# The end of a one-core attention and recurrence kernel: a chain in written order, earlier banks, ten warm-up steps

## The chip, the cores and the metric

The kernel runs on one core of a Trainium2 chip. The metric is device time in microseconds (us), the median of several runs. The engines are TensorE (PE in the profile; PEld is its weight load), VectorE (DVE), ScalarE (ACT), GpSimd (POOL) and SyncE (SP, which here only issues transfers). Each works through a queue of its own in order, and they wait for each other by semaphores. Matrix products write to PSUM[...].

## The reference

The input x has shape (4, 128, 64, 64) in float32: four batches of 128 channels and 4096 positions. Two layers are computed.

```
x = x + conv_attn(group_norm(x))          # q, k of width 64; softmax attention over 4096 positions, gated
t = tokens of x                           # (4, 4096, 128)
t = t + attn(layer_norm(t))               # q = x W, scores q q^T, softmax, weighted sum
t = t + ffn(layer_norm(t))
    # ffn: Wx = t W^T, normalised over all 4*4096 rows (batch norm),
    #      y_i = sigmoid(Wx_i + V y_{i-1}), y_{-1} = 0, over the 4096 positions in order
```

Everything is float32. The last part is a recurrence over 4096 steps for four sequences. V is orthogonal.

## The kernel before

The function `fast` does the work; a function `general` follows it, which computes everything again in a plainer way and is entered only if a test on the device fails.

The four batches run one after the other. For each batch, `layer0` computes the first attention (scores L238, exponentials L240, weighted sums L476), and `layer1` the second. In `layer1` the queries equal the keys, so the score matrix is symmetric: only blocks on and under the diagonal are computed (L795, exponentials L801), weighted directly (L672), and used a second time in transposed form, after DVE's block transposes (L642), a transfer and `reversed_products` (L685). Each of the eight blocks of 512 positions is finished by three pieces of work: `tokens` (four transposes on PE, L727; the row sums and their reciprocal, L730 to L732; products with it, L734; a layer norm, L299 to L303, whose inverse square root is taken on POOL, L145 and L146), `turn` (four transposes of the normalised rows, L747, copied by ACT, L748, and the block's result sent to HBM, L275 and L279) and `inputs` (the product with the feed-forward weight, L756; its statistics, L757; and a copy to `wxs`, L760). These pieces lie in the queue `pending`, and one is taken after each pair of score products. Block 0 of the last batch is the very last to be finished: nothing but its own chain is left then.

The order of instructions on an engine is chosen by a scheduler from priorities, except where the code asks for written order: the start of the kernel (inside `written`), and single instructions.

Then comes the recurrence. It isn't run over 4096 steps in a row: each sequence is cut into G = 128 pieces of L = 32 steps, all pieces of all four batches go forward together, and each piece begins W = 12 steps early from a zero state; since the sigmoid and V contract, the state has converged when the piece proper begins. So there are 12 + 32 = 44 steps. A step handles two halves (two batches of 128 pieces, 256 columns each): DVE preloads a PSUM bank with the scaled input (`preload`, L949, two steps ahead, three banks for each half), PE adds the product with V and the state before (L962), and ACT takes the sigmoid with the bias (L966). [...]every bank is first written by one product of PE (L926, the six marking products)[...]. Step 0 has no product: ACT takes the sigmoid of `wxs` times gain plus bias (L959). `gain` and `bias` come from the statistics of all blocks (L930 to L935). From step W + 3 on, DVE also adds the states to `t2s` (L976), one addition of 512 elements per partition for a batch and four steps; `t2s` is loaded from HBM by four transfers (L915), and when a batch is complete it is sent to the output (L981). At the end the state of each piece is compared with the state that the piece before it ended with (`gap`), and the row sums of both attentions with two bounds (`ok`, L905 to L907); if one test fails, `general` runs.

The PSUM pools of `fast` are `ps_s` (two buffers of two banks, scores), `ps_o` (three banks) and `ps_m` (one bank). The recurrence's own pool of six banks, `ps_r`, opens after these have been closed.

At the start, four warm-up products (L857, identity times the first columns of x) run while x is loaded and its statistics are taken; one more stands after the group mean (L346) and two after the group variance (L356). The first normalisation is L362, the first product of the projections L369.

Of the kernel before, what the change touches and what calls it, by code (L numbers as in the profile page):

```python
# [23 lines left out]
NT = N // P  # L24
# [8 lines left out]
PAIRS = NT // 2  # L33
LAG = 2
SHIFT = 48.0
L, W = 32, 12
G = N // L
GB = QB // L

# [133 lines left out]
def fast(  # L173
# [10 lines left out]
    bias = keep.tile([P, 1], F32, name="bias")  # L184
    first_y = keep.tile([P, 1], F32, name="first_y")

    with ExitStack() as st:
        big = st.enter_context(tc.tile_pool(name="big", bufs=1))
        ep = st.enter_context(tc.tile_pool(name="ep", bufs=4))
        accp = st.enter_context(tc.tile_pool(name="accp", bufs=1))  # L190
        work = st.enter_context(tc.tile_pool(name="work", bufs=1))
        stat = st.enter_context(tc.tile_pool(name="stat", bufs=4))
        ps_s = st.enter_context(tc.tile_pool(name="ps_s", bufs=2, space=PSUM))
        ps_o = st.enter_context(tc.tile_pool(name="ps_o", bufs=3, space=PSUM))
        ps_m = st.enter_context(tc.tile_pool(name="ps_m", bufs=1, space=PSUM))

# [96 lines left out]
        def layernorm(src, dst):  # L293

            mv = stat.tile([P, NQ, 2], F32, tag="mv", name="mv")
            rstd = stat.tile([P, NQ], F32, tag="rstd", name="rstd")
            for j in range(NQ):
                s6 = stat.tile([P, 6], F32, tag="s6", name="s6")
                nc.vector.bn_stats(s6, src[j])  # L299
                nc.vector.bn_aggr(mv[:, j, :], s6)  # L300
            inv_sqrt(rstd, mv[:, :, 1], EPS_LN)
            for j in range(NQ):
                nc.vector.tensor_scalar(  # L303
                    dst[j], src[j], mv[:, j, 0:1], rstd[:, j : j + 1],
                    ALU.subtract, ALU.mult,
                )
# [244 lines left out]
        def layer1(b, h, qt):  # L551
# [151 lines left out]
            def finish(n):  # L703
                cs = bass.ts(n, QB)
                rinv = stat.tile([P, NQ], F32, tag="rinv", name="rinv")
                t = work.tile([P, 4, NQ, 32], F32, tag="t", name="t1", bufs=2)
                if b == B - 1 and n == 0:

                    one, two = (ep.tile([P, 2, QB], F32, tag="e", name="last") for _ in range(2))
                    h2, t1 = (one[:, r, :].rearrange("q (j c) -> q j c", j=NQ) for r in range(2))  # L710
                    th = two[:, 0, :]

                    def bank():
                        return ps_s.tile([P, 2, QB], F32, tag="s", name="ml")[:, 0, :]
                else:
                    h2 = work.tile([P, NQ, C], F32, tag="h2", name="h2")
                    th = work.tile([P, QB], F32, tag="th", name="th")
                    t1 = work.tile([P, NQ, C], F32, tag="og", name="t1b")

                    def bank():  # L720
                        return ps_m.tile([P, QB], F32, tag="m", name="m1")
                nc.sync.dma_start(t, t_d[b, n])

                def tokens():
                    m = bank().rearrange("q (j c) -> q j c", j=NQ)
                    for j in range(NQ):
                        nc.tensor.transpose(m[:, j, :], oacc[:, n, bass.ts(j, P)], ident)  # L727
                    at = (B + b) * NT + n * NQ
                    den = den_all[:, at : at + NQ]
                    nc.vector.tensor_reduce(den, m, AX.X, ALU.add)  # L730
                    nc.vector.tensor_scalar(den, den, 1.0 / C, None, ALU.mult)
                    nc.vector.reciprocal(rinv, den)  # L732
                    for j in range(NQ):
                        nc.vector.scalar_tensor_tensor(  # L734
                            t1[:, j, :].rearrange("q (p i) -> q p i", p=4),
                            m[:, j, :].rearrange("q (p i) -> q p i", p=4), rinv[:, j : j + 1],
                            t[:, :, j, :], ALU.mult, ALU.add,
                        )
                    layernorm(quarters(t1), quarters(h2))

                def result():
                    turn_out(t1.rearrange("q j (p i) -> q j p i", p=4), t2_d[b, :, cs])

                def turn():
                    m = bank()
                    for j in range(NQ):
                        nc.tensor.transpose(m[:, bass.ts(j, P)], h2[:, j, :], ident)  # L747
                    nc.scalar.copy(  # L748
                        th.rearrange("c (p j k) -> c j p k", j=NQ, p=4),
                        m.rearrange("c (j p k) -> c j p k", j=NQ, p=4),  # L750
                    )
                    result()

                def inputs():
                    m = bank()
                    nc.tensor.matmul(m, lhsT=wt["f"], rhs=th, start=True, stop=True)  # L756
                    nc.vector.bn_stats(bn_st[:, b * NB + n, :], m)  # L757
                    m = m.rearrange("p (g i s) -> p i g s", i=L // 2, s=2)
                    if b == B - 1:
                        nc.vector.tensor_copy(wxs[:, :, b, bass.ts(n, GB), :], m)  # L760
                    else:
                        wx = work.tile([P, L // 2, GB, 2], F32, tag="wx", name="wx")
                        nc.vector.tensor_copy(wx, m)
                        nc.sync.dma_start(wxs_d[b, :, :, bass.ts(n, GB), :], wx)

                if b == B - 1 and n == 0:
                    pending.appendleft(tokens)
                    pending.extend([turn, inputs])
                elif b == B - 1 and n < 4:
                    pending.extend([tokens, turn, inputs])  # L770
                else:
                    pending.extend([tokens, nothing, nothing, nothing, turn, inputs])
# [66 lines left out]
                unsent.popleft()()  # L839
            while fifo:  # L840
                direct()
            pending.extend([reversed_products] * len(turned))

        def own_bank(_):
            return ps_m.tile([P, 512], F32, tag="m", name="mp")
# [8 lines left out]
        def warm(cols):  # L854

            m = ps_o.tile([P, QB], F32, tag="o", name="warm")
            nc.tensor.matmul(  # L857
                m[:, :cols], lhsT=ident, rhs=parts0[0][:, :cols], start=True, stop=True
            )

        for _ in range(4):
            warm(QB)
        for work_ in norm[:-2]:
            work_()
# [34 lines left out]
                ahead.popleft()()  # L899
        flush()  # L900


        tc.keep_in_program_order(nc.scalar.activation(first_y, shift, AF.Sigmoid))
        ok = big.tile([P, 2, 2 * B * NT], F32, tag="oacc", name="ok")
        nc.vector.tensor_scalar(ok[:, 0, :], den_all, DEN_LO, None, ALU.is_ge)  # L905
        nc.vector.tensor_scalar(ok[:, 1, :], den_all, DEN_HI, None, ALU.is_le)
        nc.vector.tensor_reduce(par_ok[:, 1:2], ok.rearrange("p a b -> p (a b)"), AX.X, ALU.min)  # L907


    with ExitStack() as st:  # L910
        scan = st.enter_context(tc.tile_pool(name="scan", bufs=1))
        ps_r = st.enter_context(tc.tile_pool(name="ps_r", bufs=1, space=PSUM))
        t2 = scan.tile([P, B, N], F32, name="t2s")
        for b in range(B):
            nc.sync.dma_start(t2[:, b, :], t2_d[b])  # L915
        y = scan.tile([P, L // 2, B, G, 2], F32, name="y")
        state = scan.tile([P, B, G + 1], F32, name="state")
        nc.gpsimd.memset(state[:, :, 0:1], 0.0)

        HB = B // 2
        banks = [[ps_r.tile([P, 512], F32, tag=f"r{s}{i}", name="ps_r") for i in range(3)] for s in range(2)]
        for s in range(2):
            for i in range(3):
                nc.tensor.matmul(  # L926
                    banks[s][i][:, : HB * G], lhsT=ident, rhs=wxs[:, 0, :HB, :, 0],
                    start=True, stop=True, skip_group_check=True,
                )
# [13 lines left out]
        def at(tile_, i, bs):  # L943
            return tile_[:, i // 2, bs, :, i % 2]
# [7 lines left out]
        preload(1)  # L952
        preload(2)
        for k, i in enumerate(steps):
            for s, bs in enumerate(halves):

                dst = state[:, bs, 1:] if k == W - 1 else at(y, i, bs)
                if k == 0:
                    nc.scalar.activation(dst, at(wxs, i, bs), AF.Sigmoid, bias=bias, scale=gain)  # L959
                    continue  # L960
                before = state[:, bs, :G] if k == W else at(y, i - 1, bs)
                nc.tensor.matmul(  # L962
# [7 lines left out]
            if k >= W:  # L970
                todo.extend((i - 3, b) for b in range(B) if i % 4 == 3)
                for j in range(len(todo) if i == L - 1 else min(1, len(todo))):
# [419 lines left out]
```

## Time and profile before

| | before |
|---|---|
| median of 3 runs | 3025.35 us (3024.1 to 3025.53) |
| profiled execution, its own time | 3023.71 us |
| its span, first to last instruction | 3021.6 us |
| PE busy | 2963.2 us, 98% of the span |
| DVE busy | 1718.1 us, 57% |
| ACT busy | 1017.0 us, 34% |
| POOL busy | 217.5 us, 7% |
| mean granted TensorE clock | 0.992 |

The profile is of one execution, so its durations belong to 3023.71 us and not to the median. In the chain of waits a line gives a start, a duration and what the end of the kernel hung on at that moment: engine, tile and line; "issue" is time in which an engine waited for nothing that the profile shows. A line of the timeline gives start, duration, engine, line, operation, output and inputs, their shapes, how many instructions were merged, and in brackets how long the engine had been idle and what released it. A line of the view by windows gives a stretch, its length, the busy time and the number of instructions of PE, PEld, DVE, ACT and POOL, then the granted clock (1.00 is full), the share of the DMA engines and GB/s. A busy PE is not PE at its peak, and a few matmul records may be missing. The ends of matmuls are modelled.

### The profile page before, as it was taken

The numbers are of one execution on the slowest core, as the hardware profiler recorded it, in microseconds if no ns is written. First come the engines' busy times: TensorE is split into PE (matmuls) and PEld (weight loads), VectorE is DVE, ScalarE is ACT, GpSimd is POOL, SyncE is SP. The second block draws the span as 40 slices with busy tenths as digits, with TensorE's granted clock in tenths as the row PEclk, the third lists the DMA queues.
The fourth block names the chain that finished last, engine by engine and source line by source line (L and its number), as shares of the span: only waits on it lengthen the run. The fifth ranks groups of instructions, "written<-read, shape, count | busy, mean of one in ns | idle before, by whom it ended". The sixth has DMA issues, their size and how long they took to land.

```text
span 3021.6 us, 32547 instructions
## 1 busy us (share of the span) xinstructions
PE 2963.2 (98%) x10768; PEld 1381.4 (46%) x10768; DVE 1718.1 (57%) x3210; ACT 1017.0 (34%) x1127; POOL 217.5 (7%) x215
## 2 busy tenths in 40 slices
PE   9999999999999999999999999999999999999985
PEld 4444444444444444444444444444444444444442
DVE  6666654544666664544466666454456666244446
ACT  3444422222344432232244443222234444222224
POOL 0011100000011100000011101000001101000000
PEclk9999999999999999999999999999999999999998
DMA  1111144334112124444311114443411113444433
GB/s 42 41 55 56 46 135 105 97 98 110 28 56 57 50 90 107 106 99 106 72 46 56 51 44 130 104 103 95 106 42 56 50 42 111 129 109 107 103 124 150
DMA packets 265425, 250.62 MB, mean 83 GB/s; under 512 B 96160, under 2 KB 180640, under 8 KB 264224
## 3 DMA queue, kind: packets, MB, share of 16 engines
q1 hardware_dynamic: 239328, 216.95, 26.6%
q10 hardware_dynamic: 25920, 31.49, 4.1%
q8 instruction: 89, 1.46, 0.2%
q14 instruction: 88, 0.72, 0.1%
HBM read 65.80 MB, written 56.62 MB: 41 GB/s over the span
## 4 chain that ended last, share of the span: by engine, by line
PE 94%; DVE 2%; DMA 2%; ACT 1%; SPq 1%; issue 0%; POOL 0%; DVEq 0%; ACTq 0%; POOLq 0%
PE o L476 29%; PE o L672 15%; PE ps L238 15%; PE ps L795 14%; PE ot L685 13%; PE o L662 1%; PE m L756 1%; PE m L267 1%; PE mp L369 1%; PE mp L438 1%; DMA tt<-dd 1%; DMA wxs<-wxs_d 1%; PE mp L423 1%; DVE t2s L976 1%; DVE ps_r L949 1%; SPq L652 1%
## 5 line engine op out<-in xcount | busy, mean ns | idle before, releaser
L476 PE MATMUL o<-e,nxt 64*128 64x512 f32 x4096 | 966.5, 589 | 0.0
L240 ACT ACTIVATE e<-ps 128x1024 f32<-128x1024 f32 x512 | 520.9, 1023 | 688.3 <-PE ps L238 648.8
L247 DVE TENSOR_TENSOR acc<-acc,e 128x1024 f32<-128x1024 f32 x448 | 548.5, 1224 | 229.3 <-ACT e L240 212.7
L476 PEld LDWEIGHTS o<-e,nxt 64*128 64x128 f32 x4096 | 400.5, 187 | 482.6 <-issue 473.8
L801 ACT ACTIVATE e<-ps,shift 128x1024 f32<-128x1024 f32 (+2 forms) x282 | 298.4, 1059 | 730.4 <-PE ps L795 417.0
L238 PE MATMUL ps<-nxt 64*128 64x512 f32 x2048 | 533.3, 595 | 1.2 <-ACT e L240 0.6
L672 PE MATMUL o<-e,h 128*128 128x512 f32 (+3 forms) x1160 | 511.0, 567 | 0.0
L795 PE MATMUL ps<-qt 128*128 128x512 f32 (+3 forms) x1128 | 502.0, 567 | 4.0 <-ACT qt L574 2.7
L642 DVE STREAM_TRANSPOSE dd<-e 128x512 f32<-128x512 f32 x444 | 287.4, 687 | 309.7 <-ACT e L801 215.8
L685 PE MATMUL ot<-tt,h 128*128 128x512 f32 x888 | 402.3, 593 | 0.0
L672 PEld LDWEIGHTS o<-e,h 128*128 128x128 f32 x1160 | 220.3, 191 | 258.5 <-issue 247.9
L795 PEld LDWEIGHTS ps<-qt 128*128 128x128 f32 x1128 | 208.3, 190 | 229.8 <-issue 207.9
L238 PEld LDWEIGHTS ps<-nxt 64*128 64x128 f32 x2048 | 195.1, 187 | 229.4 <-issue 148.8
L685 PEld LDWEIGHTS ot<-tt,h 128*128 128x128 f32 x888 | 164.4, 190 | 186.7 <-issue 185.6
L145 POOL TENSOR_SCALAR rstd<-mv 128x4 f32<-128x4 f32 x64 | 14.5, 226 | 2355.9 <-DVE mv L300 2355.9
L694 DVE TENSOR_TENSOR oacc<-oacc,ot 128x512 f32<-128x512 f32 x87 | 59.4, 682 | 161.8 <-PE ot L685 161.8
L532 DVE SCALAR_TENSOR_TENSOR t<-yt,rinv,t 128x128 f32<-128x128 f32 x128 | 36.5, 347 | 82.4 <-DMA yt<-turn_d 82.4
L543 POOL TENSOR_SCALAR h<-h 128x512 f32<-128x512 f32 x32 | 72.4, 2261 | 63.8 <-DVE d L275 61.7
L493 POOL TENSOR_SCALAR xb<-xb,bpc 128x512 f32<-128x512 f32 x32 | 58.1, 1815 | 245.5 <-DMA xb<-in_x_dram 230.2
L146 POOL TENSOR_TENSOR rstd<-rstd,mhalf 128x4 f32<-128x4 f32 x64 | 66.4, 1037 | 5.3
L381 ACT ACTIVATE nxt<-mp,par 64x512 f32<-64x512 f32 x31 | 23.9, 772 | 115.7 <-DVE nxt L377 99.8
L303 DVE TENSOR_SCALAR h<-t,mv,rstd 128x128 f32<-128x128 f32 x128 | 35.7, 343 | 46.8 <-POOL rstd L146 46.8
(159 smaller groups left out, 1583.8 us busy)
## 6 DMA issues: line engine op xcount, KB each, us to landing
tt<-dd SPq DMA_DIRECT2D x1332, 64.0 KB, 2.0
tt<-dd ACTq DMA_DIRECT2D x444, 64.0 KB, 2.0
turn_d<-d SPq DMA_DIRECT2D x384, 64.0 KB, 1.8
nxt<-in_x_dram SPq DMA_DIRECT2D x16, 512.0 KB, 5.5
xb<-in_x_dram SPq DMA_DIRECT2D x32, 256.0 KB, 3.3
t<-turn_d SPq DMA_DIRECT2D x32, 256.0 KB, 2.7
yt<-turn_d SPq DMA_DIRECT2D x32, 256.0 KB, 2.6
t_d<-t SPq DMA_DIRECT2D x32, 256.0 KB, 2.0
```

The costliest lines, as they stand in the source:

```text
L146: nc.gpsimd.tensor_tensor(dst, dst, mhalf[:, :n], ALU.pow)
L238: nc.tensor.matmul(ps[:, h, :], lhsT=lhsT, rhs=rhs, start=True, stop=True)
L240: nc.scalar.activation(e, ps, AF.Exp, scale=scale)
L247: nc.vector.tensor_tensor(acc, acc, e, ALU.add)
L476: nc.tensor.matmul(o[r], lhsT=v[rs, p + h * PAIRS, :], rhs=e[rs, h, :], start=(p == 0 and h == 0), stop=(p == PAIRS - 1 and h == 1),)
L543: nc.gpsimd.tensor_scalar(hn, hn, 1.0, None, ALU.add)
L642: nc.vector.transpose(d.rearrange("q f b k j -> q k b f j")[:, 2 * i + half], e[:, half, :].rearrange("q (b f j) -> q b f j", b=NQ, f=NQ),)
L672: nc.tensor.matmul(o[:, cols], lhsT=h[:, NQ * a + 2 * i + half, :], rhs=es, start=(a == order(n)[0] and i == 0 and half == 0), stop=(a == ...
L685: nc.tensor.matmul(ot, lhsT=h[:, NQ * n + j, :], rhs=t.rearrange("q (p b k j) -> q b k p j", p=4, b=NQ, k=NQ)[:, j], start=(j == 0), stop= ...
L694: nc.vector.tensor_tensor(oacc[:, n, :], oacc[:, n, :], o, ALU.add)
L795: nc.tensor.matmul(scores, lhsT=qt[:, bass.ts(at, P)], rhs=qt[:, n * QB + cols.start : n * QB + cols.stop], start=True, stop=True,)
L801: nc.scalar.activation(e.rearrange("p a b -> p (a b)")[:, :width], ps.rearrange("p a b -> p (a b)")[:, :width], AF.Exp, bias=shift,)
```

## The change

Eight edits, at the two ends of the kernel.

- **Order.** From the end of the last batch's loop to the first step of the recurrence, instructions stand in written order (`ordered`). The layer norm's statistics are written interleaved. With this order the block's transposition comes after its normalised rows, `bn_aggr` over all blocks before the copy of the last block to `wxs`, and the tests `ok` go to the end of the kernel.
- **Banks.** `ps_o` and `ps_m` stay open; `ps_s` is closed inside `tokens` of the last block. Four banks of the recurrence take its place, one is from `ps_o` and one from `ps_m`. They are marked at once with products of the identity and `bc`, before the layer norm's result is there.
- **The last block's banks.** Its transposes and its product use `ps_o` instead of `ps_s`.
- **Products for the clock.** Four products of 512 columns follow the marks, and four more follow the last block's product.
- **Ten warm-up steps from 1/2.** W is 10. Step 0 starts from a state of 1/2 instead of 0: its bias has V times 1/2 added (`of_half`, `first_bias`).
- **Copy.** The last block's copy to `wxs` is moved out of `inputs`, behind `bn_aggr`.
- **Block 1.** Its pieces get one empty place between `tokens` and `turn`.
- **Start.** Two warm-up products instead of four, on columns 1536 to 2047 of x instead of the first 512.

```diff
-L, W = 32, 12
+L, W = 32, 10
...
+    half = keep.tile([P, 1], F32, name="half")
+    nc.gpsimd.memset(half, 0.5)
+    first_bias = keep.tile([P, 1], F32, name="first_bias")
...
-        ps_s = st.enter_context(tc.tile_pool(name="ps_s", bufs=2, space=PSUM))
-        ps_o = st.enter_context(tc.tile_pool(name="ps_o", bufs=3, space=PSUM))
-        ps_m = st.enter_context(tc.tile_pool(name="ps_m", bufs=1, space=PSUM))
+        ps_o = keep_ctx.enter_context(tc.tile_pool(name="ps_o", bufs=3, space=PSUM))
+        ps_m = keep_ctx.enter_context(tc.tile_pool(name="ps_m", bufs=1, space=PSUM))
+        scores_ctx = ExitStack()
+        ps_s = scores_ctx.enter_context(tc.tile_pool(name="ps_s", bufs=2, space=PSUM))
...
+            sums: deque = deque()
             for j in range(NQ):
                 s6 = stat.tile([P, 6], F32, tag="s6", name="s6")
                 nc.vector.bn_stats(s6, src[j])
-                nc.vector.bn_aggr(mv[:, j, :], s6)
+                sums.append((mv[:, j, :], s6))
+                if j > 0:
+                    nc.vector.bn_aggr(*sums.popleft())
+            nc.vector.bn_aggr(*sums.popleft())
...
-                        return ps_s.tile([P, 2, QB], F32, tag="s", name="ml")[:, 0, :]
+                        return ps_o.tile([P, QB], F32, tag="o", name="ml")
...
+                    if b == B - 1 and n == 0:
+                        take_banks()
...
-                    if b == B - 1:
+                    if b == B - 1 and n == 0:
+                        last_inputs.append(m)
+                    elif b == B - 1:
...
+                elif b == B - 1 and n == 1:
+                    pending.extend([tokens, nothing, turn, inputs])
...
+            if b == B - 1:
+                ordered.enter_context(tc.manual_schedule())
             pending.extend([reversed_products] * len(turned))
...
+        def mark(m, cols):
+            nc.tensor.matmul(
+                m[:, :cols], lhsT=ident, rhs=bc.rearrange("p a c -> p (a c)")[:, :cols],
+                start=True, stop=True, skip_group_check=True,
+            )
+
+        def take_banks():
+            scores_ctx.close()
+            ps_r = keep_ctx.enter_context(tc.tile_pool(name="ps_r", bufs=1, space=PSUM))
+            for i in (1, 2):
+                for r in range(2):
+                    banks[r][i] = ps_r.tile([P, QB], F32, tag=f"r{r}{i}", name="ps_r")
+            banks[0][0] = ps_o.tile([P, QB], F32, tag="o", name="ps_r")
+            banks[1][0] = ps_m.tile([P, QB], F32, tag="m", name="ps_r")
+            for r in range(2):
+                for i in range(3):
+                    mark(banks[r][i], HB * G)
+            busy(4)
+
+        def busy(times):
+            for _ in range(times):
+                mark(banks[0][0], QB)
...
-                m[:, :cols], lhsT=ident, rhs=parts0[0][:, :cols], start=True, stop=True
+                m[:, :cols], lhsT=ident, rhs=parts0[0][:, 1536 : 1536 + cols], start=True, stop=True
             )
-        for _ in range(4):
+        for _ in range(2):
             warm(QB)
...
-        tc.keep_in_program_order(nc.scalar.activation(first_y, shift, AF.Sigmoid))
-        ok = big.tile([P, 2, 2 * B * NT], F32, tag="oacc", name="ok")
-        nc.vector.tensor_scalar(ok[:, 0, :], den_all, DEN_LO, None, ALU.is_ge)
-        nc.vector.tensor_scalar(ok[:, 1, :], den_all, DEN_HI, None, ALU.is_le)
-        nc.vector.tensor_reduce(par_ok[:, 1:2], ok.rearrange("p a b -> p (a b)"), AX.X, ALU.min)
+        of_half = banks[0][1][:, QB - 1 :]
+        nc.tensor.matmul(
+            of_half, lhsT=wt["vt"], rhs=half, start=True, stop=True, skip_group_check=True
+        )
+        busy(4)
+
+        nc.scalar.activation(first_y, shift, AF.Sigmoid)
+        nc.vector.bn_aggr(mv, bn_st.rearrange("p a b -> p (a b)"))
+        inv_sqrt(gain, mv[:, 1:2], EPS_BN)
+        nc.vector.tensor_copy(wxs[:, :, B - 1, :GB, :], last_inputs[0])
+        nc.vector.tensor_add(first_bias, of_half, col(BETA))
+        nc.vector.tensor_mul(gain, gain, col(GAMMA))
+
+        nc.vector.tensor_mul(bias, mv[:, 0:1], gain)
+        nc.vector.tensor_sub(first_bias, first_bias, bias)
+        nc.vector.tensor_sub(bias, col(BETA), bias)
...
-        ps_r = st.enter_context(tc.tile_pool(name="ps_r", bufs=1, space=PSUM))
...
-        for s in range(2):
-            for i in range(3):
-                nc.tensor.matmul(
-                    banks[s][i][:, : HB * G], lhsT=ident, rhs=wxs[:, 0, :HB, :, 0],
-                    start=True, stop=True, skip_group_check=True,
-                )
-        nc.vector.bn_aggr(mv, bn_st.rearrange("p a b -> p (a b)"))
-        inv_sqrt(gain, mv[:, 1:2], EPS_BN)
-        nc.vector.tensor_mul(gain, gain, col(GAMMA))
-
-        nc.vector.tensor_mul(bias, mv[:, 0:1], gain)
-        nc.vector.tensor_sub(bias, col(BETA), bias)
...
         for k, i in enumerate(steps):
+            if k == 1:
+                ordered.close()
...
-                    nc.scalar.activation(dst, at(wxs, i, bs), AF.Sigmoid, bias=bias, scale=gain)
+                    nc.scalar.activation(dst, at(wxs, i, bs), AF.Sigmoid, bias=first_bias, scale=gain)
...
+        ok = scan.tile([P, 2, 2 * B * NT], F32, name="ok")
+        checked = nc.vector.tensor_scalar(ok[:, 0, :], den_all, DEN_LO, None, ALU.is_ge)
+        tc.keep_in_program_order(checked)
+        nc.vector.tensor_scalar(ok[:, 1, :], den_all, DEN_HI, None, ALU.is_le)
+        nc.vector.tensor_reduce(par_ok[:, 1:2], ok.rearrange("p a b -> p (a b)"), AX.X, ALU.min)
```

In the built order of the changed kernel, the scheduler has lifted the first `ok` comparison from the end of the kernel to a place between the subtractions that give `first_bias` and `bias`, and the first preload of step 3 ahead of `first_bias`.

More of the change, by code (lines that the diff above doesn't have):

```diff
@@ L841, in layer1 @@
                 direct()
+            if b == B - 1:
+                ordered.enter_context(tc.manual_schedule())
             pending.extend([reversed_products] * len(turned))
+        HB = B // 2
+        banks = [[None] * 3 for _ in range(2)]
+        last_inputs = []
+        ordered = ExitStack()
+        def mark(m, cols):
[18 more added lines that the diff above has]
+                mark(banks[0][0], QB)
         def own_bank(_):
@@ L918, in fast @@
         nc.gpsimd.memset(state[:, :, 0:1], 0.0)
-        HB = B // 2
-        banks = [[ps_r.tile([P, 512], F32, tag=f"r{s}{i}", name="ps_r") for i in range(3)] for s in range(2)]
-        for s in range(2):
-            for i in range(3):
-                nc.tensor.matmul(
-                    banks[s][i][:, : HB * G], lhsT=ident, rhs=wxs[:, 0, :HB, :, 0],
-                    start=True, stop=True, skip_group_check=True,
-                )
-        nc.vector.bn_aggr(mv, bn_st.rearrange("p a b -> p (a b)"))
-        inv_sqrt(gain, mv[:, 1:2], EPS_BN)
-        nc.vector.tensor_mul(gain, gain, col(GAMMA))
-        nc.vector.tensor_mul(bias, mv[:, 0:1], gain)
-        nc.vector.tensor_sub(bias, col(BETA), bias)
         halves = [slice(s * HB, (s + 1) * HB) for s in range(2)]
```

## The prediction

> **What bounds the kernel now.** I read the page first, then the chain of waits over the last 100 us, the timeline there and at the start, and windows of 1 us for the clock.
>
> ```profile
> PE 2963.2 (98%) x10768; PEld 1381.4 (46%) x10768; DVE 1718.1 (57%) x3210; ACT 1017.0 (34%) x1127; POOL 217.5 (7%) x215
> PEclk9999999999999999999999999999999999999998
> ```
>
> TensorE (PE) carries the run. The diff leaves the order of the main loop on every engine as it was (apart from the names of banks), so only the two ends can move. Last 100 us of the chain of waits, in order of time (start, us, what):
>
> ```profile
> 2929.05 2.09 PE ml L756 x2
> 2931.14 0.02 issue
> 2931.17 0.70 DVE bn_st L757
> 2931.87 0.60 DVE wxs L760
> 2932.47 0.14 issue
> 2932.60 5.46 PE ps_r L926 x12
> 2938.06 0.68 PE ps_r L962 x2
> 2938.74 0.02 issue
> 2938.77 0.50 ACT y L966
> ...
> 2962.06 0.49 ACT y L966
> 2962.58 0.69 DVE t2s L976
> ...
> 2993.54 3.60 DVE t2s L976 x6
> ```
>
> Three stretches: a serial chain through the last block's layer norm and projection up to 2931; six marking products that hold the first product of the recurrence until 2938.06; then steps of 1.294 us (2938.77, 2940.06, 2941.36) until VectorE (DVE) takes over at 2962.58 and stays busy to 2997.14. The output transfers (8.4 MB near 400 GB/s) start at 2995.36 and set the end. From the timeline of that part:
>
> ```profile
> 2924.47 0.68 DVE L275 STREAM_TRANSPOSE d<-last 128x512 f32<-128x512 f32 x1
> 2927.08 1.24 PE L747 MATMUL ml<-ident,last 128*128 128x128 f32 x4 [5.89 <-DVE last L303]
> ```
>
> The transposition stands in DVE's order ahead of the last statistics; PE is idle 5.89 us. Its clock (ninth entry: PEclk):
>
> ```profile
> 2924.00:2925.00 1.00, 0.00 (x0) 0.00 (x0) 1.00 (x6) 0.00 (x0) 0.00 (x0) 0.87 0.00 0
> 2938.00:2939.00 1.00, 1.00 (x5) 0.63 (x3) 0.49 (x1) 0.23 (x1) 0.00 (x0) 0.80 1.02 434
> ```
>
> It fell to half at about 2924.74 and rose at about 2938.40. At the start of the run:
>
> ```profile
> 10.92 0.28 PE L346 MATMUL gm<-gmv,gavg 128*128 128x1 f32 x2
> 14.22 1.00 DVE L362 TENSOR_SCALAR nxt<-nxt,gdev 128x512 f32<-128x512 f32 x2 [1.24 <-PE warm L857]
> 14.82 1.13 PE L369 MATMUL mp<-nxt,w 128*128 128x512 f32 x2 [0.71 <-DVE nxt L362]
> ```
>
> The normalisation waits for a warm-up product, though its factor is ready at 13.46 (POOL, 12.88+0.58).
>
> [...]
>
> **The change part by part, tail.** Durations from the profiled execution. Its own time is 3023.71 (span 3021.6 and 2.1 around it), 1.64 under the median of the runs shown, 3025.35.
>
> 1. DVE order, up to the layer norm's result. The `ok` test leaves the gap behind the reciprocal: first-row products end 1.39 us after its start; in the block before, without `ok`, 1.34: -0.05. The transposition leaves its place before the last bn_aggr: 0.59 on the chain, less about 0.07 that this bn_aggr waits anyway: -0.52. L303 starts at 2926.10 in place of 2926.68 and its last of four ends at 2927.21.
> 2. New on PE behind the transposes that end at 2921.2: six marks of 256 columns and four products of 512. L926's twelve passes take 0.455 each at half clock, so 0.228 at full; a 512 pass is 0.43: 12x0.228 + 8x0.43 = 6.2. They end near 2927.2, just as L303 is done[...]. The four transposes then take 0.6 (block before: 0.60 to 0.66) in place of 1.24. ACT's copy: 2927.8 in place of 2928.42: -0.6. Bounds: -0.8 (products end earlier), 0 (they run 0.6 longer; each us more is a us on the path).
> 3. L756 at full clock is 1.10 (2898.71) in place of 2.08: -0.98. bn_stats starts at 2929.6.
> 4. bn_aggr goes ahead of the copy of wxs: 2931.17 to 2934.40 (gain times gamma) was 3.23; 0.74 + 2.03 = 2.77 remains: -0.46. The copy (0.60) and the new addition (0.16) lie under POOL's 0.97. The first state starts at 2933.3 in place of 2935.39. The one-column product with V is unseen before; the nearest, L346, took 0.28; it and four more products (3.4) run on PE until 2933.1, before the state is there: 0. The sigmoid table's load (1.28) follows ACT's copy and is over by 2929.7: 0.
> 5. No marks remain between: the first recurrence product starts when ACT has written the state, 0.6 later, 2933.9; its activation at 2934.7 against 2938.77: **-4.1** for items 1 to 5.
> 6. Ten warm-up steps: two of 1.294 us, all before DVE is the bound: **-2.6**. The first addition to t2s moves from 2957.40 to 2950.7.
> 7. From there DVE does the same 32 additions (0.59) and 52 preloads (0.39). In its built order the third addition stands behind six preloads, no longer four: DVE idles about 0.8 where it idled 0.2: **+0.6**. It ends at 2991.1.
> 8. `ok`, `is_le` and its reduction move into the shadow of the output transfers (about 20 us): 0, and 0.9 without that cover.
>
> Queues: one `ok` test was lifted between first_bias and bias on DVE, where it waits for all stores to t2_d; behind it stand bias and the preloads of steps 1 and 2. Those four stores now follow the transposition at 2927.8; before, they had landed 3.05 after it: 2930.8. The test is reached near 2933.1: 2.3 us in hand. SP issues the same four loads of t2s behind the stores, near 2931 as now (2931.20); block 0 lands 6.4 after, needed at 2950.7; block 3 by 2954.3, needed near 2963. POOL: a 0.10 memset at the start, before its first wait; the memset of `state` moves behind the gain, needed ten steps later: 0. Four bank pools open sooner; no product in the built order waits for them. Tail: 4.1 + 2.6 - 0.6 = **6.1 off**, bounds 5.0 and 6.9.
>
> **Start.** Two warm-up products instead of four, from the second transfer (no later than 6.27: the third bn_stats starts there without a wait), and on columns that the first normalisation doesn't write. PE is free near 9.8; L346 starts at 10.6: -0.3. The normalisation no longer waits for PE: 13.2 in place of 14.22. PE frees at 13.7, the first product at 13.8: **-1.0**, if the clock is up by 10.6 as now (spacing of weight loads falls from 0.85 to 0.43 after 9.5). But the new stretch is only 3.5 us long, followed by a hole to 10.6[...]. Then the next three products run at half clock: first product at 15.5, **+0.7**. [...] I take -1.0, slightly likelier; both ends stay in the range.
>
> Sum: -7.1. On the profiled execution 3016.6; on the median 3025.35 - 7.1 = **3018.3**.
>
> **Rivals.**
> - A, the clock comes late at the start: tail -6.1, start +0.7: 3020.0. For it: the 3.5 us stretch. [...]
> - B, the gain is handed back to DVE: an addition stands in its queue before its t2s block landed, or preloads stall behind the bursts of three additions. For it: DVE was the bound for the last 34 us, and its built order now has such a burst. Against it: 9 to 13 us between landing and need. It keeps about half: 3022.
> - C, slower: the clock products become the path. PE's queue is in order; if it ran them at half clock, 6.2 would be 12.4, the last transposes would wait until 2933.4 (+6.3 against 2927.1), the second four (6.8 in place of 3.4) would hold the recurrence until about 2943, and the activation of step 1 would stand near 2944.6, 5.9 late; less 2.6 for two steps, plus 0.6: 3029. It decides from about 3 us of added PE time at both places together beyond what is hidden. Against it: the clock is 1.00 at 2921 with no pause ahead.
> - D, it doesn't do what it says: ten steps from 1/2 leave a state further than 2^-18 from its successor and the general path runs, at least doubling the time. A sigmoid's slope is at most 1/4 and V is orthogonal; 0.25^10 is 9.5e-7, a quarter of 2^-18 for a deviation of 1. One in a hundred.
>
> **How the numbers follow.** Forecast 0.45 (own range 3017.0 to 3019.6), A 0.36, B 0.10, C 0.05, D 0.01, the rest unnamed small losses. A measurement can tell about 0.2%, 6.05 us: the bound is 3019.3. The forecast passes it nine times in ten, A one in four: 0.41 + 0.09 = 0.50 faster; slower is C, D and a little: 0.06; within it 0.44. Range: from the forecast with a tail of 6.9 and the profiled execution's luck, 3016.4, to B, 3021.9.
>
> **What would show it.** Right: transposes of the last block over 0.6 us at PEclk 1.00 from 2921 on; first recurrence activation near 2934.7 (less the start's gain); DVE's additions ending 6.1 earlier relative to the start of the last block; first product near 13.8. A: that product after 15 with weight loads 0.85 apart at 11 to 13. B: idle time of DVE before L976's successor put to a transfer. C: a wait of the last transposes on PE's own queue. Wrong altogether: a granted clock of 0.50 between 2921 and 2935, or a changed main loop.

## The result and the profile after

| | before | after |
|---|---|---|
| median | 3024.48 us (9 runs, 3023.0 to 3025.85) | 3016.22 us (9 runs, 3013.84 to 3019.02) |
| ratio | | 0.9974, interval 0.9966 to 0.9983 |
| profiled execution, its own time | 3023.71 us | 3015.99 us |
| its span | 3021.6 us | 3014.3 us |

The change takes off 8.26 us in the medians (the interval is 5.1 to 10.3) and 7.72 in the two profiled executions. From the page of the changed kernel, busy time and the granted clock in 40 slices:

```profile
PE 2961.1 (98%) x10774; PEld 1378.9 (46%) x10774; DVE 1716.2 (57%) x3208; ACT 1016.1 (34%) x1123; POOL 223.1 (7%) x216
PEclk9999999999999999999999999999999999999998
```

Nothing shows there but six more passes of PE (10774 for 10768; each float32 product counts here as two: in the timeline below, the product of L378 into `mp` stands as x2). The chain of waits (start, us, what) shows the end:

```profile
2919.00 0.70 DVE oacc L703
...
2920.40 6.03 PE ps_r L873 x20
2926.42 0.45 PE ml L758 x4
...
2926.95 0.60 ACT last L759
...
2927.59 1.12 PE ml L767 x2
...
2932.50 0.62 ACT y L1003
...
2933.18 0.72 PE ps_r L1006 x2
...
2933.92 0.49 ACT y L1010
...
2986.69 3.60 DVE t2s L1020 x6
```

The marks and clock products of L873 are done at 2926.42, and the four transposes follow without a pause: 0.45 on the chain (0.60 in the timeline) in place of 1.24. The product with the feed-forward weight (L767) takes 1.12 for 2.08. The first product of the recurrence comes 0.7 after ACT starts on the first state, no longer behind 5.46 us of marks. The windows (PE's busy time is the second number, the granted clock the last but two) say that the clock held, at 1.00:

```profile
2926.00:2928.00 2.00, 1.27 (x6) 0.69 (x5) 1.10 (x3) 1.03 (x2) 0.00 (x0) 1.00 0.01 4
2932.00:2934.00 2.00, 1.19 (x4) 0.59 (x4) 2.00 (x8) 1.20 (x3) 0.00 (x0) 1.00 0.81 311
```

The start, from the timeline of the changed kernel:

```profile
6.50 3.38 PE L908 MATMUL warm<-nxt,ident 128*128 128x512 f32 x4 [6.50 <-DMA nxt<-in_x_dram]
10.79 0.35 PE L355 MATMUL gm<-gmv,gavg 128*128 128x1 f32 x2 [0.91 <-DVE gmv L353]
13.44 1.00 DVE L371 TENSOR_SCALAR nxt<-nxt,gdev 128x512 f32<-128x512 f32 x2 [0.52 <-POOL gdev L146]
14.04 1.13 PE L378 MATMUL mp<-nxt,w 128*128 128x512 f32 x2
```

At the start the granted clock tells nothing: the windows print 1.00 from the first slice on, also where passes are twice as long as later. So a late clock at the start is read here from the passes. In this profile the weight loads of the warm-up passes lie 0.85 us apart at first (7.49 and 8.34) and 0.43 later (12.60 and 13.03). The one product after the group mean took 1.10 us here and 2.06 with the start alone, below; in the tail, L767 took 1.12 at a granted clock of 1.00 and 2.09 at 0.50 (without both sets of four, below). So in this execution the clock was up in time. The normalisation waits for POOL and no longer for PE, and the first product comes at 14.04 for 14.82. That 0.78 is carried to the end: the last addition to `oacc` in block 0 stands at 2919.00 for 2919.80, in the chain before:

```profile
2919.80 0.70 DVE oacc L694
```

Below, times of the tail are counted from that addition, which takes the start out: DVE's additions to `t2s` end at 77.34 before and 71.29 after, 6.05 earlier. The parts are -4.05 up to step 1's activation (18.97 to 14.92), -2.6 by two steps less, and +0.59 from the first addition to the end of the last (39.74 to 40.33).

The second comparison of `ok` (L1031), which the scheduler had lifted (the section on the change calls it the first), started at 2932.32 and waited for nothing.

### The profile page after: what moved, and what is told of

Same layout as the page of the kernel before. It is cut to its first block, busy times and chain, and to the rows that moved or that the text cites. A ratio compares the mean times of both kernels' runs of the same rounds, so it can differ in the third digit from the quotient of the medians.

```text
span 3014.3 us, 32549 instructions
## 1 busy us (share of the span) xinstructions
PE 2961.1 (98%) x10774; PEld 1378.9 (46%) x10774; DVE 1716.2 (57%) x3208; ACT 1016.1 (34%) x1123; POOL 223.1 (7%) x216
## 4 chain that ended last, share of the span: by engine, by line
PE 94%; DVE 2%; DMA 1%; ACT 1%; SPq 0%; issue 0%; ACTq 0%; POOL 0%; DVEq 0%
PE o L485 29%; PE o L681 15%; PE ps L243 15%; PE ps L810 14%; PE ot L694 13%; PE o L671 1%; PE m L272 1%; PE m L767 1%; PE mp L378 1%; PE mp L447 1%; DMA wxs<-wxs_d 1%; PE mp L432 1%; DVE t2s L1020 1%; DVE ps_r L991 1%; PE mq L582 1%; PE m L736 1%
```

## The experiments

**The parts apart: the tail alone, the start alone.** The tail alone is the changed kernel with this start:

```diff
-                m[:, :cols], lhsT=ident, rhs=parts0[0][:, 1536 : 1536 + cols], start=True, stop=True
+                m[:, :cols], lhsT=ident, rhs=parts0[0][:, :cols], start=True, stop=True
...
-        for _ in range(2):
+        for _ in range(4):
             warm(QB)
```

> The changed kernel with its start put back: four warm-up products on the first columns, as before; the tail is as changed. Theory S (the parts add: start -0.8, tail and output -7.3 or so, against a median of 3024.5 before and 3016.2 after): first product back near 14.8, the start of the last block's addition back near 2919.8, time about 3017.1, 0.9976 of before. Rival L (the two warm-up products bring the clock up in some runs only, so that the start is worth about 0 in the mean): time within 0.4 of the changed kernel's 3016.2, and a spread of its runs of some 3 us like before's 2.9, against 5.2 seen for the changed kernel.

The start alone is the kernel before with the same lines the other way round.

> The kernel before with the new start alone. Theory S: first product near 14.0, everything behind it 0.8 earlier, tail as before; time about 3023.7 (-0.8), spread some 3 us. Rival L: a mean gain near 0 and a spread of 4 us or more, with single runs slower than before by up to 0.7.

Measured: the tail alone 3016.65 (ratio 0.9975, 0.9966 to 0.9984), the start alone 3024.6 (1.0000, 0.9992 to 1.0008). The tail alone gives -7.8, the whole gain as far as these runs tell. The start alone shows no gain, as rival L said; but its interval is 2.4 us wide to either side, so the medians alone don't rule out theory S's -0.8. L's other half, the spread, didn't tell: with 37 runs the kernel before spreads over 5.1 us too. What speaks for L is the profiled execution of the start alone (PE in the timeline):

```profile
6.33 3.75 PE L857 MATMUL warm<-nxt,ident 128*128 128x512 f32 x4 [6.33 <-DMA nxt<-in_x_dram]
10.86 0.56 PE L346 MATMUL gm<-gmv,gavg 128*128 128x1 f32 x2 [0.77 <-DVE gmv L344]
11.28 2.06 PE L857 MATMUL warm<-nxt,ident 128*128 128x512 f32 x2
13.12 0.42 PE L356 MATMUL gv<-gdev,gavg 128*128 128x1 f32 x2
13.41 2.95 PE L857 MATMUL warm<-nxt,ident 128*128 128x512 f32 x4
16.20 1.02 PE L369 MATMUL mp<-nxt,w 128*128 128x512 f32 x2
```

This is rival A of the prediction: the same two products, 0.17 us earlier than in the changed kernel's profile, and by the passes the clock did not come up in time. The single product after the group mean takes 2.06 in place of 1.10, and the first product of the projections comes at 16.20, 5.34 us after the group mean. Eight profiled executions have the new start (the changed kernel, this one, and six below): six have the first product at 13.93 to 14.21, two at 16.20 and 16.44. Their mean is 14.63, against 14.82 and 14.87 with the old start. So, as far as eight draws tell, the start brings about 0.2: six times it gains 0.6 to 0.9, twice it costs 1.4 to 1.6.

**One warm-up product, and three early ones.** The changed kernel with `range(1)`:

> The changed kernel with one of the two warm-up products at the start left out; no part of the result depends on it. It prices the late clock (rival A of the prediction): [...]the clock comes up only after the three products that follow the group mean. Expected: weight loads 0.85 apart at 11 to 13, first product near 15.5 in place of 14.04, time about 3017.7 (+1.5 on the changed kernel). If the clock comes up all the same, first product near 14.0 and time 3016.2.

The changed kernel with three warm-up products on other columns:

```diff
-                m[:, :cols], lhsT=ident, rhs=parts0[0][:, 1536 : 1536 + cols], start=True, stop=True
+                m[:, :cols], lhsT=ident, rhs=parts0[0][:, 512 : 512 + cols], start=True, stop=True
...
-        for _ in range(2):
+        for _ in range(3):
```

> The changed kernel with three warm-up products, on the second 512 columns of the first transfer: they start as early as the four of the kernel before (near 5.1) and end near 9.9, and the first normalisation, which writes the first 512 columns first, still waits for no product. Theory S: as the changed kernel, 3016.2, first product near 14.0 or up to 0.1 earlier. Rival L: the late clock is gone from all runs, median 0.3 to 0.7 lower (3015.7) and a spread near 3 us.

Measured with one: first product at 16.66, time 3018.41, 2.2 over the changed kernel. A late clock costs 2.2 to 2.6 against an early one, not the 1.5 that I had from rival A. The stretch from the group mean to the first product was taken too short there: 4.9 us (10.6 to 15.5), against 5.34 with the start alone and 5.92 here. Three products at half clock are six passes of 0.85 (the spacing measured at the start), which is 5.1 already, and the two one-column products among them take 0.7 more (0.42 and 0.29 in the profile above). With three early: first product 14.07 (14.03 and 14.17 in the two kernels below that share this start), spread 3.6 us, median 3016.58; the gain in the median (0.3 to 0.7) is not seen, and is below what these runs can tell.

**Steps.** The changed kernel with `L, W = 32, 12`:

> The changed kernel with twelve warm-up steps instead of ten; they still start from 1/2. Item 6 of the prediction says that a step costs 1.294 us and that both steps taken out lay ahead of the point from which VectorE is the bound: the first addition to t2s and the end of the additions 2.6 later, counted from the last block's addition, so 74.1 (from 71.3) for its end, and a time near 3019.0 (+2.6 on the changed kernel's 3016.4, the mean of its median and of the run with three warm-ups). Rival: VectorE's queue takes part of it back (the built order has two additions in a row less), and the end moves by 2.0 or less: 3018.4.

End of the additions 73.90, for 71.29: +2.60, as item 6 has it. The median rose more, to 3020.5 (21 runs, 3017.74 to 3023.51). The tail of the profiled execution shows no more than the 2.60; the rest is scatter of the kind described below, or open.

**Products for the clock.** Without both sets of four (the two calls `busy(4)` taken out):

> The changed kernel without both sets of four products for the clock; the six marks stay where the change put them, and no part of the result depends on the eight. Theory (items 2 and 3: they hold the clock): TensorE idles for 4 us at about 2922 and again at 2929, the clock falls to half, the four transposes take up to 1.24 and the product with f up to 2.08, and the first steps of the recurrence run at half clock: activation of step 1, counted from the last block's addition, 16.0 to 18.0 in place of 14.9, time 3017.6 to 3019.5. Rival (they are not needed, and only delay the transposes): the clock stays up and the transposes start up to 0.4 earlier: 14.6, time 3016.1.

Without the second set alone:

> The changed kernel without the second set of four products alone (those behind the product with V, under the last statistics); the first set stays. Theory K (the second set keeps the clock for the recurrence): TensorE is idle for 4 us from 2928.8, the clock falls in that gap, and the first two or three steps run at half clock: activation of step 1 at 15.3 to 16 from the last block's addition in place of 14.9, end of the additions 1.0 to 1.5 later, time 3017.4 to 3018. Theory Z (the gap is too short for the clock to fall in most executions): 14.9, time 3016.4, and no half clock in the trace.

With eight in the first set (`busy(8)`):

> The changed kernel with eight products for the clock instead of four behind the six marks. It prices rival C of the prediction, which held that each microsecond by which these products outlast the layer norm is a microsecond on the path. In the trace of the changed kernel they end 0.6 after the first quarter of the layer norm's result is there, and the last quarter is there 0.05 later, so their slack is used up: four more products of 0.86 make 3.4. Expected: activation of step 1 at 18.1 to 18.4 from the last block's addition in place of 14.9, end of the additions 74.3 to 74.8 in place of 71.3, time 3019.6. Rival: the wait is partly hidden by another (POOL's gain, the table load), and less than 2.5 arrives.

| counted from the last block's addition | step 1's activation | end of additions | median |
|---|---|---|---|
| before | 18.97 | 77.34 | 3024.48 |
| after | 14.92 | 71.29 | 3016.22 |
| without both sets | 16.61 | 74.05 | 3019.53 |
| without the second set | 15.53 | 72.41 | 3018.52 |
| eight in the first set | 18.42 | 74.78 | 3021.52 |

Without both, the granted clock was 0.50 from 2927.5 to 2941.15, and the chain of waits shows it: L758 1.26 for 0.45 and L767 2.09 for 1.12.

```profile
2927.10 1.26 PE ml L758 x4
...
2929.07 2.09 PE ml L767 x2
```

Without the second set, the windows show it fall at 2929.2, 0.9 us after PE's last product, and stay down until 2936.0, past step 1's activation at 2933.94:

```profile
2928.00:2930.00 2.00, 0.24 (x3) 0.16 (x1) 1.80 (x3) 0.45 (x2) 0.00 (x0) 0.79 0.36 84
2932.00:2934.00 2.00, 1.29 (x3) 1.13 (x4) 1.76 (x6) 1.10 (x3) 0.00 (x0) 0.50 0.92 385
```

The eight products are worth 2.76 us on the path, the second four alone 1.12. In both traces the expectation for the clock held, and "not needed" fell. With eight in the first set, 3.44 us more of products came through as 3.49 at the end; the chain shows the transposes behind them:

```profile
2919.26 9.46 PE ps_r L873 x28
2928.72 0.45 PE ml L758 x4
```

So rival C had its slope right, one for one, and the size chosen (four) stands near the point from which it costs: in the changed kernel the products end at 2926.42, and the last quarter of the normalised rows at 2926.48. The medians rose by 3.3, 2.3 and 5.3 in the three runs, each more than its trace shows (2.76, 1.12 and 3.49), as with twelve steps; that rest is open.

**DVE's order.** The changed kernel with the additions and preloads pinned:

```diff
-                    nc.vector.tensor_scalar(bank(k, s), at(wxs, steps[k], bs), gain, None, ALU.mult)
+                    made = nc.vector.tensor_scalar(bank(k, s), at(wxs, steps[k], bs), gain, None, ALU.mult)
+                    if W + 2 <= k < W + 18:
+                        tc.keep_in_program_order(made)
...
+                    if k < W + 15:
+                        tc.keep_in_program_order(added)
```

> The changed kernel with VectorE's additions to t2s and its preloads of the steps from W to W+17 held in written order, so that an addition never stands behind more than two preloads. Item 7 of the prediction (the built order makes VectorE idle 0.8 where it idled 0.2): end of the additions 0.5 to 0.6 earlier, counted from the last block's addition: 70.7 in place of 71.3; time 3015.8. Rival: the idle time is set by ScalarE's steps, which VectorE must wait for in any order, and only moves: 71.2 to 71.4, time 3016.4.

In the changed kernel DVE is idle before its first addition and twice more behind it, because its third addition stands behind six preloads that wait for ScalarE (DVE in the timeline):

```profile
2949.96 0.69 DVE L1020 TENSOR_TENSOR t2s<-t2s,y 128x512 f32<-128x512 f32 x1 [0.31 <-ACT y L1010]
...
2951.94 1.64 DVE L991 TENSOR_SCALAR ps_r<-wxs,gain 128x256 f32<-128x256 f32 x4
2953.84 1.02 DVE L991 TENSOR_SCALAR ps_r<-wxs,gain 128x256 f32<-128x256 f32 x2 [0.26 <-ACT y L1010]
2955.13 0.69 DVE L1020 TENSOR_TENSOR t2s<-t2s,y 128x512 f32<-128x512 f32 x1 [0.27 <-ACT y L1010]
```

In written order there is no idle time after the first addition:

```profile
2951.51 0.69 DVE L1022 TENSOR_TENSOR t2s<-t2s,y 128x512 f32<-128x512 f32 x1 [0.30 <-ACT y L1012]
...
2954.27 0.68 DVE L1022 TENSOR_TENSOR t2s<-t2s,y 128x512 f32<-128x512 f32 x1
```

End of the additions 70.43: 0.86 earlier, more than the 0.5 to 0.6 expected. All of it lies at these six preloads: from 2951.94 to 2955.13 they take 3.19 us, where six take 2.33 in written order. Of it 0.53 are the two idle times (0.26 and 0.27); the rest is the preload pair between them, whose second starts 0.53 and not 0.39 behind the first, and the ends of the two instructions ahead of the waits, about 0.1 each, by which the next one otherwise overlaps them (a preload lasts 0.48 and the next instruction starts 0.39 behind it). The time, 3016.82, can't show 0.86.

**A hole that both kernels have.** Laid side by side, the traces run level to 0.1 us for most of the way and part at few places: the start, the beginning of the last layer in the first batch (from 386 to 426 us PE's waits over 0.2 add up to 1.30 in the one and 2.61 in another; not followed up), and near 2580. There PE waits in the last batch for the first `tt`, which is queued on SP behind the three loads of `wxs` (timeline of the changed kernel; SPq is an issue of a transfer):

```profile
2551.70 9.62 SPq L947 DMA_DIRECT2D wxs<-wxs_d  x3
2562.24 16.74 SPq L661 DMA_DIRECT2D tt<-dd  x12
...
2580.47 2.90 PE L671 MATMUL o<-tt,h 128*128 128x384 f32 x6 [2.65 <-DMA tt<-dd]
```

The hole is 2.65 to 3.21 us long in the eleven traces that have it. In each of them the granted clock falls to 0.50, and it stays there for 3.41 us or for 6.83. The changed kernel had 6.83 and the one with three early products 3.41; both were level within 0.03 us at 2577, and stand at 2919.00 and 2917.42 at the last block's addition. The kernel before had 6.83 as well, with a wait of 3.10: 0.45 more of waiting, and about 0.4 less lost at half clock, where PE worked for 5.14 us and not 5.97. That the start's 0.78 came through whole is the luck of this pair. So the loads were spread, twelve pieces of 512 KB, one in three steps of the last layer:

```diff
                 for i in range(B - 1):
-                    nc.sync.dma_start(wxs[:, :, i, :, :], wxs_d[i])
+                    for r in range(4):
+                        rs = bass.ts(r, L // 8)
+                        loads.append(
+                            lambda rs=rs, i=i: tc.keep_in_program_order(
+                                nc.sync.dma_start(wxs[:, rs, i, :, :], wxs_d[i][:, rs])
+                            )
+                        )
...
                         elif ahead:
                             ahead.popleft()()
+                        if loads and clock > 15 and clock % 3 == 0:
+                            loads.popleft()()
```

> The changed kernel with the three loads of wxs (2 MB each), which stand on SP's queue ahead of the first loads of tt in the last batch, cut into twelve and spread over that batch's blocks. All traces so far show TensorE idle for 2.65 us near 2577.8 while it waits for tt, then half clock for 3.4 or 6.8 us, in the changed kernel and the kernel before alike. If the loads cause that: no hole and no half clock there, the last block's addition at 2914 to 2915.5 in place of 2919.0 (start alike), time 3011 to 3012.5. If the hole has another cause, or the spread loads delay later tt loads as much: 3016.4, the same half clock near 2580.

This with three early warm-up products and DVE in written order:

> All that helped together: the loads of wxs spread, three warm-up products on the second 512 columns at the start, VectorE's additions held in written order. If the parts add (-4.5, 0 to -0.7 by a clock that is up in every run, -0.9): 3010.5, first product near 14.1, end of the additions 70.4 from the last block's addition, a spread of the runs under 4 us. If the loads of wxs bring nothing: 3015.2.

The hole near 2580 and its half clock are gone in both, but the first gave 1.0 us and not 4 (3015.25), for PE had two new waits of 1.27 us, one of them again for a `tt`. Behind this one the clock fell again, at 2836.08, for 3.41 us (timeline and windows of the kernel with spread loads):

```profile
2835.36 2.19 PE L671 MATMUL o<-tt,h 128*128 128x384 f32 x6 [1.27 <-DMA tt<-dd]
...
2836.00:2838.00 2.00, 2.00 (x6) 1.43 (x5) 1.92 (x4) 0.00 (x0) 0.00 (x0) 0.52 0.46 112
```

The combined kernel measured 3012.84 (0.9966, 0.9955 to 0.9978), with the same two waits (1.41 and 1.25) and no half clock there: its six passes with the `tt` that came late take 1.54, not 2.19. The last run took the pieces in twelve steps in a row (`if loads and clock > 15:`).

> The combined kernel with the twelve pieces of wxs loaded in twelve steps in a row from the sixteenth step of the last layer on, in place of one in three. In the combined kernel TensorE has two new waits, 1.41 us at 2835 for tt and 1.25 us at 2882 for ScalarE. If the pieces that stand in SP's queue until 2814 cause them, they go, and the time is 3010.3 (the combined kernel's 3012.8 less 2.5). If they come from the changed order of TensorE's products, which the planner chose anew, they stay: 3012.8.

Both waits are gone, and the first product with `tt` has none (timeline of this kernel):

```profile
2568.15 1.46 PE L671 MATMUL o<-tt,h 128*128 128x384 f32 x6
```

PE's idle times over 0.25 us from 2540 up to the one for the last block's addition add up to 3.30, for 6.19 in the changed kernel. The time is 3009.59 (5 runs, 3008.65 to 3010.56; 0.9951, 0.9938 to 0.9965), 6.6 under the changed kernel (on another chip; the kernel before took 3024.04 there). The planner ordered PE's products anew here too, which speaks for the pieces in SP's queue and not for a new order as such. This version, with three edits at once, beats both kernels.

## Why the prediction was right, and where it wasn't

The forecast was -7.1, 3018.3 on the median shown then; -8.26 was measured. As a difference that lies within the stated range; as a time, 3016.22 is 0.2 under its lower end, for over nine runs the kernel before takes 3024.48 and not 3025.35. The direction and the mechanism of the tail were right, the start's size was not, and about 1 us lay where the sum didn't look.

- **Items 1 to 5** hold nearly to the digit. With the start's 0.80 added back: the normalised rows start at 2926.16 (forecast 2926.10), the twenty products end at 2927.22 (2927.2), ACT's copy starts at 2927.75 (2927.8), the statistics of the block at 2929.56 (2929.6), the first state at 2933.30 (2933.3), step 1's activation at 2934.72 (2934.7). Apart from the products for the clock, these edits (order, earlier marks, the copy moved) were not taken out one by one: their shares are read from this one trace.
- **Item 2's condition**, that each microsecond more is one on the path, was measured at 3.49 for 3.44. That no stretch loses the clock was measured on both sides: the granted clock is 1.00 in the changed kernel from 2586.44 to 2989.21, and 0.50 in the tail with the products taken out. Why it holds there was not shown.
- **Item 6**: 2.60 for 2.6, by the run with twelve steps.
- **Item 7**: +0.59 for +0.6, from the first addition to the end of the last. Written order saves 0.86 and not 0.59, as it takes out the idle time of the kernel before too (39.46 for the stretch, under the 39.74 there); my expectation for that run forgot the 0.2 that the item starts from. DVE's additions end at 2991.09 with the 0.80 (forecast 2991.1).
- **Item 8** and the queues: `ok` is hidden, its lifted comparison waited for nothing, and the loads of `t2s` were issued at 2930.36.
- **Outside the sum**: from the end of the additions to the end of the span took 24.46 before and 24.74 with the start alone, but 23.5 to 24.3 in eleven of the twelve profiles with the new tail (25.3 in the other); the time around the span fell from 2.1 and 2.0 to 1.7 to 1.8 in all but one. The sum held both unchanged. That makes 0.9 more in the changed kernel's own profile and some 1.3 in most others, and with it the tail's -6.05 comes near the -7.8 of the run with the tail alone. The output transfers are issued from 1.8 us ahead of the end of the additions in both kernels; the slowest of the four took 21.8 and 22.1 us to land with the old tail, 20.8 to 21.3 in ten of the twelve with the new one (22.0 and 22.6 in the others). Why they land sooner is open; no run looked at it.
- **The start is the step that failed.** I took -1.0 and gave rival A 0.36, +0.7 as its price. What A foresaw, a late clock, happened in two of eight executions by their passes; why in these two was not shown. Its price was +1.4 to +1.6: the group mean came at 10.86, not 10.6, and the stretch to the first product took 5.34 and not 4.9, because six passes at half clock (5.1) and two one-column products (0.7) don't go into 4.9 even when the clock rises before their end (in the run with the start alone the last four passes took 2.79, not 3.4). When the clock is up the gain is 0.8 and not 1.0 (the group mean came at 10.79). In the mean of the eight that is -0.2. The sum took the likelier of two outcomes where it needed their mean: the prediction's own chances for the two, 0.45 and 0.36 (estimates of mine, which no trace gave), and its sizes give about -0.2 (an estimate). That this agrees with the eight is luck, for both sizes and the chances were off.
- **Rivals B, C and D** did not happen. B had a real part, the 0.59 that DVE's order cost, but no addition waited for a transfer.

The forecast's total thus was near for a mixed reason: 0.8 too much at the start against 1.9 too little behind the additions, around the span and in what remains between traces and medians.

## What to carry to other kernels

Fill a serial stretch on TensorE with products that end just when its next input is ready: here the granted clock was 1.00 with them and 0.50 without, they were worth 2.76 us, and 3.44 us of products beyond that point cost 3.49. A gain that hangs on the clock coming up at a certain moment was a draw here, won in six of eight executions (first product at 13.93 to 14.21) and lost in two (16.20 and 16.44); price both outcomes and take the mean, or start the warm-up earlier (with three products from about 5.2 us on the first product came at 14.03 to 14.17 in all three traces taken, too few to say always). When executions of one kernel differ, lay their traces side by side by a fixed instruction: the places where they part point to the holes that are worth closing, and bulk loads queued ahead of small urgent ones were the cause here (a wait of 2.65 us behind them, none with the loads in small pieces).

## What was not expected of the hardware

Sixteen stretches with a granted clock of 0.50 were seen up to the end of the recurrence. Each lasted 3.41, 6.83 or 13.65 us (within 0.02):

| PE's pause | traces | length of the pause, us | clock at 0.50 for, us |
|---|---|---|---|
| before the first `tt`, near 2580 | 11 | 2.65 to 3.21 | 3.41 in seven, 6.83 in four |
| before the last block's transposes, tail as before | 2 | 5.89 in the kernel before | 13.65 |
| at the same place, without both sets of four | 1 | 2.8 | 13.65 |
| before the recurrence, without the second set | 1 | 4.45 | 6.83 |
| before a later `tt`, with spread loads | 1 | 1.27 | 3.41 |
| before the same `tt`, combined kernel | 1 | 1.41 | not at all |

The length of the pause alone doesn't tell these apart: 1.27 us were followed by half clock, and 1.41 us in another kernel were not. Nor did the fall come at one place in a pause. It came 3.5 us after PE's last product in the kernel before and 0.9 us after it without the second set; near 2580 it came between 1.69 us before PE's next product (the kernel before) and 1.25 us behind its start (the tail alone). And work did not bring the clock back at once: behind the hole near 2580, PE worked for 5.14 us at 0.50 in the kernel before, and for 5.97 in the changed one. What decides these moments is open; no run looked at it. The ends of matmuls are modelled and a few records can be missing, so the pauses are good to a few hundredths at best.
